# Self attention of layer 0: the values of fifteen elements from seven block products instead of eight

## The chip, the cores and the metric

The kernel runs on one core of a Trainium2 chip. The metric is the device time of one execution in microseconds; times shown are medians of several executions. Besides these there is one profiled execution, whose trace tells when every instruction and every transfer ran. Its times count from the first instruction (the span).

## What is computed

A batch of 16 elements x, each 256 positions by 256 features in fp32, goes through two transformer layers. Each layer has a self attention, a cross attention and a feed-forward part, so there are six phases of 16 elements. The change touches only the first phase, the self attention of layer 0, and in it the matrix product that makes the values:

```python
def _attn(xq, ctx, wq, wkv, wo, bo):          # self attention: ctx is xq
    q = _heads(xq @ wq)
    k, v = jnp.split(ctx @ wkv, 2, axis=-1)   # v: 256 x 1024 for each element
    ...
    o = jnp.einsum('bhnm,bhmd->bhnd', softmax(q k^T / 8), v)
    return o @ wo + bo
```

For one element the values are [256 x 256] times [256 x 1024]: the normalized and modulated input, held transposed as hT, times wv.

## The kernel before

**Order.** Every engine's order is written out by hand: what a function issues for an engine runs on it in just this order. The main loop goes through steps; an attention element has two (s = 0 and s = 1), and each step takes care of two groups of four heads. In a step of layer 0 TensorE makes, for the next step, the keys and queries (`stage_rotary`, L82 by way of the helper `product`), then the weighted sums of the values (`layer0_sums`, L638), in step 0 the values of the next element (`layer0_values`), in step 1 the folded output product of the element before (`finish_folded`), and at last the scores of the next step (`stage_s`, L569).

**Values.** `layer0_values(nxt)` in step 0 makes eight block products of 128 x 128 by 128 x 512: two halves t of the positions, two halves of the 1024 columns, two halves k of the 256 features, the last two added up in PSUM. `product` splits each into four matmuls of 32 output rows, which run side by side; the profile records each of these as two matmuls and two weight loads. The four results stand in the PSUM banks 6, 7, 4 and 5, and ScalarE copies each to the tile v (L478).

**Banks.** The scores of a step write banks 0 to 3 (first group of heads) and then 4 to 7 (second group). Keys and queries of the first group use banks 0 and 1, those of the second 2 and 3; the weighted sums use 4 and 5.

**VectorE in step 0**, in order: `both` (L590, a sum of two parts of the exponentials, two SBUF inputs), a transpose (L596), `m` (L526, keys and queries times the rotary table, read from PSUM), more of the same, the row sums (L603), and then `prepare_moments(third)`: the statistics of the element three further on (L324 to L328; the last is `ve`). For a cross attention to come, `context_moments` does the same for the context.

**POOL (GpSimd)**, in order: `qk` (L534, from pairs of m; m has two buffers of each kind, so m of the next group waits for qk), in step 0 `scale` (L627) and part of `fold_inner` (L736), in step 1 `add_bias` (L423) and one half of hT of the element two further on (L397, `prepare_input`; ScalarE makes the other half, L396). Once in the phase, in step 1 of element 0, `fold_weights` (L727) makes five sums of wo for the folded output product.

**SP** issues all transfers. The output weights wo of a phase come from the pool tag "wo" with two buffers; those of the cross attention (wo_ca, 1 MB) are loaded in step 1 of element 1, in the part "early".

**Start.** Before the loop, element 0 is prepared and its values and scores made; then come the moments, transposes and inputs of elements 1 and 2, with `prepare_input(jobs[1])` as the last call.

## Time and profile before

| what | time, us |
| --- | --- |
| median of 3 runs | 2196.24 (2194.89 to 2197.59) |
| the profiled execution | 2198.64 |
| its span, first to last instruction | 2196.8 |
| granted TensorE clock over the span | 0.999 |
| one usual element of the first phase | 41.3 |
| values of one element, TensorE (160.00 to 166.98) | 6.98 |

How each engine is used in two usual elements, from the busy times of the stretches 77.4 to 118.7 and 118.7 to 160.0 (each of 41.3 us):

| engine | first stretch, us | second stretch, us |
| --- | --- | --- |
| PE (TensorE, matmuls) | 41.30 | 41.30 |
| PEld (TensorE, weight loads) | 26.26 | 26.29 |
| DVE (VectorE) | 34.71 | 31.82 |
| ACT (ScalarE) | 12.73 | 12.73 |
| POOL (GpSimd) | 27.76 | 25.71 |

A line of the timeline reads: start, duration, engine, source line, operation, output<-inputs, shapes, how often in a row; in brackets the idle time of the engine before it and what ended that. [...] In the list of waits a line reads: who <- whom, total us, how many, the longest.

### The profile page before, as it was taken

How to read it: one execution, taken by the hardware profiler on the slowest of the kernel's cores; microseconds unless marked ns; L12 is line 12 of the kernel's file. 1: busy time of each engine (PE TensorE's matmuls, PEld its weight loads, DVE VectorE, ACT ScalarE, POOL GpSimd, SP SyncE). 2: the span in 40 equal slices, each digit the busy share in tenths (PEclk: the TensorE clock that was granted, in tenths of full speed). 3: DMA queues.
4: the chain of work that ended last, by engine and by line, in shares of the span. 5: the costliest groups of instructions: out<-in, count | busy, mean ns of one | idle time of the engine just before them, and what ended most of it. 6: DMA issues, size and time to landing. Idle time of an engine off the chain costs nothing.

```text
span 2196.8 us, 110836 instructions
## 1 busy us (share of the span) xinstructions
PE 2180.7 (99%) x50505; PEld 1431.6 (65%) x50505; DVE 1660.6 (76%) x3120; ACT 837.5 (38%) x1307; POOL 1071.6 (49%) x1033
## 2 busy tenths in 40 slices
PE   9999999999999999999999999999999999999998
PEld 5666666666665666666665668776656656657887
DVE  5886776777788899888899876664777777777654
ACT  3323323323233333333323332234666666663322
POOL 3766656656657867676676752221222232222220
PEclk9999999999999999999999999999999999999999
DMA  6110110110132221221212123221221232223221
GB/s 192 47 39 22 24 40 23 24 41 22 26 85 72 67 65 35 47 54 40 60 35 59 26 71 88 46 54 29 62 43 42 55 93 59 62 52 86 61 62 37
DMA packets 309321, 117.83 MB, mean 54 GB/s; under 512 B 245652, under 2 KB 292073, under 8 KB 308713
## 3 DMA queue, kind: packets, MB, share of 16 engines
q1 hardware_dynamic: 308840, 110.64, 21.1%
q8 instruction: 397, 6.50, 1.2%
q14 instruction: 84, 0.68, 0.1%
HBM read 77.14 MB, written 33.29 MB: 50 GB/s over the span
## 4 chain that ended last, share of the span: by engine, by line
PE 91%; DVE 3%; POOL 2%; DMA 1%; issue 1%; SPq 0%; ACT 0%; DVEq 0%; POOLq 0%; ACTq 0%
PE banks L82 59%; PE banks L569 15%; PE banks L638 9%; PE banks L654 5%; PE banks L505 1%; PE banks L472 1%; DVE m L526 1%; POOL raw L627 1%; POOL qk L534 1%; DMA spread<-sums_seen 0%; POOL folded L736 0%; DMA sums_seen<-inv 0%; DVE both L590 0%; DVE rows L603 0%; DVE squares L596 0%
## 5 line engine op out<-in xcount | busy, mean ns | idle before, releaser
L581 ACT ACTIVATE pr<-banks 128x1024 f32<-128x1024 f32 x576 | 487.6, 937 | 416.7 <-PE banks L569 211.5
L534 POOL TENSOR_TENSOR qk<-m,m 128x512 f32<-128x512 f32 x256 | 347.5, 1377 | 307.7 <-DVE m L526 199.6
L526 DVE TENSOR_TENSOR m<-banks,rope 128x512 f32<-128x512 f32 x512 | 324.2, 679 | 86.4 <-POOL qk L534 80.8
L590 DVE TENSOR_TENSOR both<-pr 128x512 f32<-128x512 f32 x256 | 222.7, 884 | 107.7 <-ACT pr L581 107.4
L645 ACT COPY raw<-banks 128x512 f32<-128x512 f32 x128 | 75.1, 587 | 468.6 <-PE banks L638 443.3
L569 PE MATMUL banks<-qk 32*64 32x256 f32 x8192 | 241.4, 378 | 4.0 <-DVE x L753 2.8
L638 PE MATMUL banks<-pr,v 128*32 128x256 f32 x4096 | 233.2, 379 | 0.0
L569 PEld LDWEIGHTS banks<-qk 32*64 32x64 f32 x8192 | 184.9, 131 | 64.6 <-issue 28.7
L704 ACT ACTIVATE g<-banks,cols 128x256 f32<-128x256 f32 x256 | 106.4, 472 | 273.0 <-PE banks L82 261.4
L638 PEld LDWEIGHTS banks<-pr,v 128*32 128x32 f32 x4096 | 132.9, 110 | 88.6 <-ACT pr L581 0.7
L82 PE MATMUL banks<-folded_w,folded 128*32 128x128 f32 x5856 | 176.2, 273 | 1.7 <-POOL folded L736 1.1
L627 POOL TENSOR_TENSOR raw<-raw,spread 128x512 f32<-128x512 f32 x128 | 162.8, 1304 | 19.0 <-DMA spread<-sums_seen 17.7
L82 PEld LDWEIGHTS banks<-folded_w,folded 128*32 128x32 f32 x5856 | 164.0, 110 | 3.1 <-POOL folded L736 2.2
L596 DVE STREAM_TRANSPOSE squares<-both 128x1024 f32<-128x1024 f32 x128 | 159.4, 1245 | 4.4
L603 DVE TENSOR_REDUCE rows<-squares 128x32 f32<-128x1024 f32 x128 | 155.5, 1215 | 2.2
L689 POOL TENSOR_TENSOR oT<-oT,spread 128x256 f32<-128x256 f32 x64 | 45.7, 736 | 209.8 <-DVE spread L688 209.8
L654 PE MATMUL banks<-pr,wide_v 128*32 128x256 f32 x2048 | 134.4, 379 | 1.1 <-ACT pr L581 1.1
L82 PE MATMUL banks<-hT,wk_sa 128*32 128x256 f32 x2048 | 135.3, 382 | 0.0
L330 POOL TENSOR_TENSOR rstd<-ve,neg_half 128x2 f32<-128x2 f32 x95 | 73.3, 772 | 125.9 <-DVE ve L328 122.5
L423 POOL TENSOR_TENSOR x<-x,bo_b 128x256 f32<-128x256 f32 x96 | 73.2, 782 | 125.8 <-DVE xh L338 125.8
L82 PE MATMUL banks<-hT,wq_ca 128*32 128x256 f32 x2048 | 133.9, 379 | 0.0
L82 PE MATMUL banks<-hT,wq_sa 128*32 128x256 f32 x2048 | 133.9, 379 | 0.0
(162 smaller groups left out, 3667.0 us busy)
## 6 DMA issues: line engine op xcount, KB each, us to landing
turned<-blocks SPq DMA_DIRECT2D x380, 64.0 KB
fetched<-turned SPq DMA_DIRECT2D x380, 64.0 KB
spread<-sums_seen SPq DMA_DIRECT2D x128, 128.0 KB
x<-in_x SPq DMA_DIRECT2D x16, 256.0 KB
fetched_c<-turned_c SPq DMA_DIRECT2D x64, 64.0 KB
cT<-in_ctx_turned SPq DMA_DIRECT2D x16, 256.0 KB
out<-x SPq DMA_DIRECT2D x16, 256.0 KB
ctx<-in_ctx SPq DMA_DIRECT2D x16, 192.0 KB
```

Of the source, the lines that this page charges most:

```text
L82: nc.tensor.matmul(out[cut], lhsT[:, cut], rhs, start=start, stop=stop)
L526: nc.vector.tensor_tensor(m, pq, rope[:, s : s + 1, :].to_broadcast([P, 2, N]), ALU.mult)
L534: nc.gpsimd.tensor_tensor(r, x, y, (ALU.subtract, ALU.add)[out])
L569: nc.tensor.matmul(banks[64 * g : 64 * g + 64, at + h, t * N : (t + 1) * N], lhs, rhs, start=(half == 0), stop=(half == 1 or job["layer"] ...
L581: nc.scalar.activation(pr[:, one], sc[:, one], AF.Exp, scale=0.125 if job["layer"] == 0 else 0.25)
L590: nc.vector.tensor_tensor(job["both"][:, 2 * p : 2 * p + 2, :], pr[:, :, 0, :], pr[:, :, 1, :], ALU.add)
L596: nc.vector.transpose(job["squares"].rearrange("p b k -> p (b k)"), job.pop("both").rearrange("p h n -> p (h n)"))
L603: nc.vector.tensor_reduce(job["rows"][:, u, :], job.pop("squares"), AX.X, ALU.add)
L627: nc.gpsimd.tensor_tensor(part, part, spread[:, u : u + 1, :].to_broadcast([P, 2, N]), ALU.mult)
L638: nc.tensor.matmul(o[32 * h : 32 * h + 32, half, :], v[:, t, col : col + 32], prs[h // 2][:, h % 2, t, :], start=(t == 0), stop=(t == NT - 1),
L654: nc.tensor.matmul(o[32 * h : 32 * h + 32], v[:, t, 4 * c + h, 32 * e : 32 * e + 32], prs[h // 2][:, h % 2, t, :], start=(t == 0), stop=(t ...
L704: nc.scalar.activation(g[:, c, :], ph[:, c, :], AF.Gelu, bias=column(w["b1"], 2 * u + c))
```

## The change

The values of elements 1 to 15 are made by Strassen's method in Winograd's form. With a[t][k] the four 128 x 128 blocks of the input and b[k][h] the four 128 x 512 blocks of the weights, seven products give the four blocks of v:

- Once, before the loop, POOL makes four sums of the weights (`split_value_weights`, t1 to t4, each 128 x 512). They lie in a buffer of the tag "wo".
- For each element POOL makes four sums of the input blocks (`split_value_inputs`, s1 to s4, each 128 x 128): for element 1 before the loop, for the others in step 1, two elements ahead, right after `prepare_input(after)`.
- TensorE makes seven products (`split_values`) in place of eight. Four of them are added up one after another in bank 6 (main), and ScalarE copies what stands there after each of the four; between them stand the products into banks 4, 7 and 5.
- VectorE then adds those three banks to what ScalarE copied: four additions of 128 x 512 (`join`), called after the statistics of step 0.
- The load of wo_ca moves from step 1 of element 1 to step 1 of element 14, behind the values' weights of the cross attention, since its buffer now first holds the split weights.
- Element 0 and the cross attention keep `layer0_values`.

```diff
-    def product(out, lhsT, rhs, start, stop):
+    def product(out, lhsT, rhs, start, stop, read_between=False):
...
-            nc.tensor.matmul(out[cut], lhsT[:, cut], rhs, start=start, stop=stop)
+            nc.tensor.matmul(out[cut], lhsT[:, cut], rhs, start=start, stop=stop, skip_group_check=read_between)
...
             w["wv"] = wtile([P, 2, H * 64], "wv", f"wv_{kind}")
+            if kind == "sa":
+                w["split_v"] = wtile([P, 8, D], "wo", "split_v", 2)
...
+        if part == ("early" if kind == "sa" else "output"):
             w["wo"] = wtile([P, 8, D], "wo", f"wo_{kind}", 2)
             nc.sync.dma_start(out=w["wo"], in_=chunked(a[f"{kind}_wo"]))
...
+    def split_value_weights():
+        b = value_weights()
+        t1, t2, t3, t4 = phases[0]["split_v"] = [phases[0]["w"]["split_v"][:, 2 * i : 2 * i + 2, :].rearrange(
+            "p c d -> p (c d)") for i in range(4)]
+        nc.gpsimd.tensor_tensor(t1, b[0][1], b[0][0], ALU.subtract)
+        nc.gpsimd.tensor_tensor(t2, b[1][1], t1, ALU.subtract)
+        nc.gpsimd.tensor_tensor(t3, b[1][1], b[0][1], ALU.subtract)
+        nc.gpsimd.tensor_tensor(t4, b[1][0], t2, ALU.subtract)
+
+    def split_value_inputs(job):
+        if job["p"] > 0 or job["b"] == 0:
+            return
+        a = value_inputs(job)
+        t = work.tile([P, 4, P], F32, tag="value_sums", name=f"value_sums_{job['key']}", bufs=1)
+        s1, s2, s3, s4 = job["split_v"] = [t[:, i] for i in range(4)]
+        nc.gpsimd.tensor_tensor(s1, a[1][0], a[1][1], ALU.add)
+        nc.gpsimd.tensor_tensor(s2, s1, a[0][0], ALU.subtract)
+        nc.gpsimd.tensor_tensor(s3, a[0][0], a[1][0], ALU.subtract)
+        nc.gpsimd.tensor_tensor(s4, a[0][1], s2, ALU.subtract)
+
+    def split_values(job):
...
+        main, other, side, extra = (bank(i, 512) for i in (6, 7, 4, 5))
+        for at, left, right, first, kept in (
+            (main, a[0][0], b[0][0], True, v[0][0]), (side, s1, t1, True, None), (main, s2, t2, False, v[0][1]),
+            (other, a[0][1], b[1][0], True, None), (main, s3, t3, False, v[1][1]), (extra, s4, b[1][1], True, None),
+            (main, a[1][1], t4, False, v[1][0]),
+        ):
+            product(at, left, right, first, True, True)
+            if kept is not None:
+                nc.scalar.copy(kept, at)
+
+        def join():
+            for to, at in ((v[0][0], other), (v[0][1], side), (v[1][1], side), (v[0][1], extra)):
+                nc.vector.tensor_tensor(to, at, to, ALU.add)
+        return join
...
     prepare_input(jobs[1])
+    split_value_inputs(jobs[1])
+    split_value_weights()
     for i, (j, s) in enumerate(steps):
...
             load_phase(job["p"] + 1, "values")
+            if job["p"] == 0:
+                load_phase(1, "output")
...
+            joins = None
             if nxt["kind"] == "attn" and s == 0:
-                layer0_values(nxt)
+                if nxt["p"] == 0:
+                    joins = split_values(nxt)
+                else:
+                    layer0_values(nxt)
             if s == 0:
                 prepare_moments(third)
                 context_moments(third)
+                if joins:
+                    joins()
                 prepare_fetch(after)
             else:
                 prepare_norm(third)
                 prepare_context(third)
                 prepare_input(after)
+                split_value_inputs(after)
                 if job["b"] == 0:
                     fold_weights(job["phase"])
```

More of the change, by code (lines that the diff above doesn't have):

```diff
@@ L478, in layer0_values, with value_weights, value_inputs @@
                 nc.scalar.copy(job["v"][:, t, cut], pv)
+    def value_weights():
+        return [[phases[0]["w"]["wv"][:, k, h * 512 : (h + 1) * 512] for h in range(2)] for k in range(2)]
+    def value_inputs(job):
+        return [[job["kT"][:, k, t * P : (t + 1) * P] for k in range(2)] for t in range(2)]
+    def split_value_weights():
[6 more added lines that the diff above has]
+        nc.gpsimd.tensor_tensor(t4, b[1][0], t2, ALU.subtract)
@@ new lines, in split_values @@
+    def split_values(job):
+        a, b = value_inputs(job), value_weights()
+        s1, s2, s3, s4 = job.pop("split_v")
+        t1, t2, t3, t4 = phases[0]["split_v"]
+        job["v"] = work.tile([P, NT, H * 64], F32, tag="v", name=f"v_{job['key']}")
+        v = [[job["v"][:, t, h * 512 : (h + 1) * 512] for h in range(2)] for t in range(2)]
+        main, other, side, extra = (bank(i, 512) for i in (6, 7, 4, 5))
[11 more added lines that the diff above has]
+        return join
```

## The prediction

> **What bounds the kernel now.** I read the engine totals first, then the chain that ended last, then TensorE's own waits in the first 660 us (the self attention of layer 0), then the order of time around three of its elements.

> ```profile
> PE 2180.7 (99%) x50505; PEld 1431.6 (65%) x50505; DVE 1660.6 (76%) x3120; ACT 837.5 (38%) x1307; POOL 1071.6 (49%) x1033
> PE 91%; DVE 3%; POOL 2%; DMA 1%; issue 1%; SPq 0%; ACT 0%; DVEq 0%; POOLq 0%; ACTq 0%
> PE banks L136 <- POOL ones L95: 1.3, 1, 1.3
> PE banks L154 <- DMA rows<-in_rows: 0.2, 1, 0.2
> ```

> TensorE is the bound, and up to 660 us it waits for nobody but at the very start. So a product taken away there is worth its full time, and a new wait of TensorE costs its full time: there is no slack to absorb it.

> ```profile
> 160.00 7.05 PE L82 MATMUL banks<-wv_sa,hT 128*32 128x512 f32 x64
> 161.29 0.13 PEld L82 LDWEIGHTS banks<-wv_sa,hT 128*32 128x32 f32 x4 [0.30 <-issue]
> 161.72 0.13 PEld L82 LDWEIGHTS banks<-wv_sa,hT 128*32 128x32 f32 x4 [0.30 <-issue]
> 161.97 0.59 ACT L478 COPY v<-banks 128x512 f32<-128x512 f32 x1 [1.13 <-PE banks L82]
> 164.02 0.64 DVE L328 TENSOR_SCALAR ve<-mv 128x2 f32<-128x2 f32 x1
> 166.98 3.71 PE L569 MATMUL banks<-qk 32*64 32x256 f32 x128
> 170.16 1.92 DVE L590 TENSOR_TENSOR both<-pr 128x512 f32<-128x512 f32 x2 [5.50 <-ACT pr L581]
> ```

> This is a usual element (times from 160.00 on; the stretch of 41.3 us repeats). The eight products take 6.98. Each is 8 recorded matmuls in two quartets; weight loads come in quartets 0.4285 apart, each issued when the quartet before starts. VectorE has finished its statistics (ve) at 4.66 after the values' start and is then idle for 5.5: the room for the joins. Their deadline is the second half of the scores, which writes banks 4 to 7: it starts 1.8 into the scores, at 8.76 now.

> **The gain.** One product of eight: 2 x 0.4285 = 0.857 us in 15 elements, 12.9 us. The four ScalarE copies stay four.

> **Waits on the reused bank.** Products 3, 5 and 7 overwrite what a copy is still reading. From a main product's second quartet on: 0.61 until its last matmul ends (0.59 and three steps of 0.006), 0.07 until the copy starts (161.90 to 161.97), 0.586 the copy, 0.05 to the weight load that waits (VectorE's end at 685.75, TensorE at 685.80): 1.316. TensorE would be free after three quartets, at 1.286. It is 0.03 late, and a weight load that is not issued ahead adds some 0.03 (the first quartets after such a wait stand 0.03 to 0.05 further apart). Products 3 and 5 also wait for POOL's sums; a second wait in an instruction of its own cost 0.06 more in these rows (VectorE ends 684.73, matmul 684.88):

> ```profile
> 684.88 0.61 PE L569 MATMUL banks<-qk 32*64 32x256 f32 x2 [0.99 <-DVE x L753]
> 685.80 0.91 PE L569 MATMUL banks<-qk 32*64 32x256 f32 x24 [0.31 <-DVE x L757]
> ```

> So 0.05 to 0.14 a wait; I take 0.075, as it is open whether the copy's wait is the separate one: 45 x 0.075 = 3.4 us (2.3 to 6.3). A usual element then saves 0.857 - 0.225 = 0.63 before its scores, and the joins' deadline moves from 8.76 to 8.13.

> **The joins.** Four additions from PSUM, 128x512, like m (four in 2.54). ScalarE's copies and products 4 and 6 end before their turn (the third copy near 5.3). In a usual element: 4.66, plus 0.3 because POOL's first new sum slips between the two `both` additions (`both` took 0.91 beside POOL's hT and 0.69 without it), plus 2.54, plus 0.1 to TensorE: 7.6, half a microsecond before 8.13. Hidden by the 5.5 of idle time: 0 in 11 elements. Elements 14 and 15 also have the context's statistics there, which end at 6.01: 6.01 + 0.3 + 2.54 + 0.1 = 8.95, 0.8 late, twice: 1.6 us (1.0 to 2.6).

> **POOL's sums, and where they stand in the queue.** An input sum is 128x128. 128x512 takes 1.25 and 128x256 0.70 (four in 2.79), so the line gives 0.43 and four make 1.7; bounds: in proportion 0.32 each, 1.3, and as 128x256, 2.8. They run after hT of an element, where POOL next idles 5.7, so usually they are hidden (without that room qk, m and the joins would slip by the 1.7, and the joins' half microsecond with it). A weight sum is 1.26 alone (2.52 for two) and 1.43 beside VectorE (7.15 for five): 5.0, to 5.7. All eight stand, once, behind hT of element 1 and ahead of its qk:

> ```profile
> 37.19 0.95 POOL L397 TENSOR_SCALAR hT<-fetched,fac_a,add_a 128x256 f32<-128x256 f32 x1 [5.79 <-DVE m L526]
> 38.11 2.52 POOL L534 TENSOR_TENSOR qk<-m,m 128x512 f32<-128x512 f32 x2
> 39.42 2.54 DVE L526 TENSOR_TENSOR m<-banks,rope 128x512 f32<-128x512 f32 x4 [1.71 <-POOL qk L534]
> 46.53 0.17 DVE L328 TENSOR_SCALAR ve<-mv 128x2 f32<-128x2 f32 x1
> 49.15 3.71 PE L569 MATMUL banks<-qk 32*64 32x256 f32 x128
> ```

> qk slips by 6.7 (6.3 to 8.5). VectorE's m waits for qk's buffers, and behind m in VectorE's queue stand the reductions, the statistics and the joins: 46.70 + 6.7 + 2.54 + 0.1 = 56.05 at TensorE, where the second scores would start at 49.15 + 1.82 - 0.63 = 50.34. **Loss 5.7** (5.3 to 7.5). The products themselves have their operands in time (t4 near 45, used at 47.5).

> The next element has a queue that is late already, for fold_weights stands ahead of qk, and now four input sums ahead of that:

> ```profile
> 69.53 7.15 POOL L727 TENSOR_TENSOR folded_w<-wo_sa 128x512 f32<-128x512 f32 x5
> 76.64 2.52 POOL L534 TENSOR_TENSOR qk<-m,m 128x512 f32<-128x512 f32 x2
> 77.37 7.05 PE L82 MATMUL banks<-wv_sa,hT 128*32 128x512 f32 x64
> 85.06 0.63 DVE L328 TENSOR_SCALAR ve<-mv 128x2 f32<-128x2 f32 x1
> ```

> The statistics end 8.32 after the values' start; plus 1.7 for the sums, less 0.35 that VectorE gains on TensorE during the first stall (its first m of the next step came 2.33 after the scores' end, and needs only 1.97 for TensorE's product), plus 2.54 and 0.1: 12.3 against 8.13. **Loss 4.2** (3.8 to 5.3). From the third element on the stall itself has given POOL its time back.

> [...]

> **What is moved.** wo_ca (1 MB) is issued at element 14 behind wv_ca instead of at 80.9 us, since its buffer first holds the split weights. Both wait on SP's queue for the same last products (wv_ca now leaves at 621.60). Behind them SP next issues turned at 644.14; at the span's mean 54 GB/s the megabyte takes 19 us and is through by then, and its first reader is POOL at 727.5: 0. If it were not, turned would come up to a few us late against hT, which is wanted an element later. The flag of the product helper issues nothing.

> **Sum.** -12.9 + 3.4 + 5.7 + 4.2 + 1.6 = +2.0 us on the profiled span of 2196.8, 2198.8; that execution took 2198.64 in all, 1.8 outside the span, and stands 2.4 above the median 2196.24 of the runs shown. The forecast for the median is 2196.24 + 2.0 = 2198.3. With every cost at its low end -0.5, at its high end +8.8: 2195.7 to 2205.0 for this case alone.

> **Rivals.**
> - Joins late in every element (slower). Place: the second scores of the 11 usual elements. It decides from 0.5 us of lateness on. For it: `both` may be held by two of the new sums rather than one (0.75 instead of 0.3), and four separate 0.69 additions with a wait each make 3.0 instead of 2.54: 4.66 + 0.75 + 3.0 + 0.1 = 8.5, 0.4 late, 11 x 0.4 = 4.4, and some 2.2 more in the other four: +8.6, 2204.8. Against: m keeps its 0.61 step beside POOL.
> - POOL's new work is covered (faster): no stall in elements 1 and 2, 2.0 - 9.9 = -7.9, 2188.4. For it: POOL idles 5.79 just before 37.19, and wv_sa is there since 21 us. Against: the sums stand behind hT in program order, and qk follows hT at once.
> - The copies are the bound (slower): 0.25 a wait, 45 x 0.25 = 11.3 instead of 3.4, +9.9, 2206.1. For it: nothing is spare on that path (0.03 short as it is), and ScalarE copies raw just before. Against: that copy ends at 160.85, before the first one can start.

> **How the numbers follow.** The case of the sum 0.60, joins late 0.16, covered 0.12, copies 0.12. Within 0.2% (about what a measurement here can tell from no change) is 2191.9 to 2200.6. The first case ends there with 0.40, above with 0.19, below with 0.01; joins late is above with 0.15; covered is below with 0.11; copies above with 0.10; the rest within. Faster 0.12, same 0.44, slower 0.44; the time is that of the likeliest case, so no change that can be told. The range 2190 to 2207 reaches into the rivals on both sides and leaves out about 2 in 10.

> **What will show it.** Right: seven products in about 6.35 us per element; TensorE waiting on VectorE's new line about 5 and 4 us in elements 1 and 2, under 1 in 14 and 15, and not at all between; three waits on ScalarE's copies of some 0.1 each; POOL's first qk near 45 instead of 38. Wrong: no wait at 50 us, qk near 38, waits on the joins in every element, or gaps of 0.25 and more between the products.

## The result, and the profile after

The changed kernel takes 2203.18 us (median of 9 runs, 2200.66 to 2204.58) against 2196.24 us (9 runs, 2194.61 to 2197.59): a ratio of 1.0031, 95% interval 1.0021 to 1.0041, so 6.9 us slower. The forecast was 2198.3 with a range of 2190 to 2207. Its profiled execution took 2204.2 us, with a span of 2202.4 and a mean granted clock of 0.998. The functions below the change have moved down: scores are L627 now (L569 before), qk is L592, m L584, both L648, ve L331, the sums of inputs L511 to L514, those of the weights L500 to L503, the copies of the products L531 and the joins L535.

First the busy times and the chain that ended last, from the page:

```profile
PE 2178.8 (99%) x50385; PEld 1435.3 (65%) x50385; DVE 1706.6 (77%) x3180; ACT 836.8 (38%) x1307; POOL 1116.9 (51%) x1097
PE 89%; DVE 4%; POOL 3%; DMA 2%; issue 1%; SPq 1%; ACT 0%; DVEq 0%; POOLq 0%; ACTq 0%
```

TensorE has 120 matmul records less and is still the bound, but its share of the chain fell from 91 to 89%: VectorE, POOL and a transfer each have a point more. TensorE's own waits up to 660 us (who, whom, total us, how many, longest) say where:

```profile
PE banks L627 <- DVE v L535: 8.1, 2, 4.7
...
PE banks L82 <- POOL split_v L500: 0.7, 1, 0.7
PE banks L627 <- DVE m L584: 0.6, 1, 0.6
...
PE banks L82 <- POOL split_v L501: 0.3, 1, 0.3
```

Two waits of the scores on the joins, and three small ones before the first of them (on sums of the weights and on m). None of these was there before. The timeline of element 1, all engines, from the landing of its input to the next keys:

```profile
39.86 0.60 ACT L399 ACTIVATE hT<-fetched,add_a,fac_a 128x256 f32<-128x256 f32 x1 [6.09 <-DMA fetched<-turned]
40.61 0.47 POOL L511 TENSOR_TENSOR value_sums<-hT 128x128 f32<-128x128 f32 x1
...
43.72 1.06 PE L82 MATMUL banks<-split_v,value_sums 128*32 128x512 f32 x8 [0.71 <-POOL split_v L500]
...
47.45 2.52 POOL L592 TENSOR_TENSOR qk<-m,m 128x512 f32<-128x512 f32 x2
...
48.76 2.53 DVE L584 TENSOR_TENSOR m<-banks,rope 128x512 f32<-128x512 f32 x4 [11.26 <-POOL qk L592]
...
55.86 0.17 DVE L331 TENSOR_SCALAR ve<-mv 128x2 f32<-128x2 f32 x1
55.94 2.48 DVE L535 TENSOR_TENSOR v<-banks,v 128x512 f32<-128x512 f32 x4
...
57.98 4.15 PE L627 MATMUL banks<-qk 32*64 32x256 f32 x64 [4.66 <-DVE v L535]
...
62.06 1.07 PE L82 MATMUL banks<-hT,wk_sa 128*32 128x256 f32 x16
```

This is read from top to bottom: POOL's eight sums take 6.84 (40.61 to 47.45), VectorE has stood idle for 11.26 until qk frees its buffers, its statistics end at 55.86, the joins follow, and the second half of the scores starts at 57.98. The last two rows show something more: that half takes 4.08 (57.98 to 62.06; its row's 4.15 runs 0.07 into the next), where the same work took 1.86 before. Some of that is a wait inside it: it starts after the third of the four joins, and goes on in earnest 0.55 later, when the fourth has ended (58.42). The table of stretches of 5 us (busy times of PE, PEld, DVE, ACT and POOL, then the granted clock, the third number from the end) shows the rest:

```profile
50.00:55.00 5.00, 2.72 (x64) 1.50 (x60) 4.93 (x7) 2.09 (x3) 2.50 (x2) 1.00 0.00 0
55.00:60.00 5.00, 2.02 (x34) 1.29 (x42) 4.93 (x12) 0.34 (x1) 0.70 (x1) 0.85 0.00 0
60.00:65.00 5.00, 5.00 (x102) 2.77 (x90) 1.77 (x3) 1.94 (x2) 0.00 (x0) 0.81 0.01 3
```

TensorE's clock fell. The trace's clock records put it at 0.5 from 58.52 to 61.94, and once more from 99.48 to 102.90, after the second wait; before the change no such record stands between 15 and 2192 us. The second wait is in element 2 (timeline of POOL, VectorE and TensorE, and the stretch of 5 us with the lowest clock):

```profile
80.47 7.16 POOL L785 TENSOR_TENSOR folded_w<-wo_sa 128x512 f32<-128x512 f32 x5
87.59 2.52 POOL L592 TENSOR_TENSOR qk<-m,m 128x512 f32<-128x512 f32 x2
...
96.49 2.47 DVE L535 TENSOR_TENSOR v<-banks,v 128x512 f32<-128x512 f32 x4
...
98.51 3.84 PE L627 MATMUL banks<-qk 32*64 32x256 f32 x64 [3.43 <-DVE v L535]
102.27 1.35 PE L82 MATMUL banks<-hT,wk_sa 128*32 128x256 f32 x16
```

```profile
100.00:105.00 5.00, 5.00 (x94) 2.71 (x82) 2.84 (x3) 1.94 (x2) 4.26 (x4) 0.71 0.02 5
```

And a usual element, in order of time:

```profile
174.04 1.04 PE L82 MATMUL banks<-wv_sa,hT 128*32 128x512 f32 x8
...
174.90 2.05 PE L82 MATMUL banks<-split_v,value_sums 128*32 128x512 f32 x16
...
175.15 0.59 ACT L531 COPY v<-banks 128x512 f32<-128x512 f32 x1 [0.27 <-PE banks L82]
...
176.74 1.07 PE L82 MATMUL banks<-wv_sa,hT 128*32 128x512 f32 x8
...
178.22 0.61 DVE L331 TENSOR_SCALAR ve<-mv 128x2 f32<-128x2 f32 x1
...
178.74 2.47 DVE L535 TENSOR_TENSOR v<-banks,v 128x512 f32<-128x512 f32 x4
...
180.49 3.71 PE L627 MATMUL banks<-qk 32*64 32x256 f32 x128
```

The joins end at 181.21, before the second half of the scores needs their banks, and the scores run through in 3.71, as before: the joins are hidden. The products take 6.45 (174.04 to 180.49) instead of 6.98. The element's period is 40.79 instead of 41.32.

The time by which the changed kernel's trace lags behind that of before, at the values of one element after another, is -0.2 at element 1, +9.3 at element 2, +14.6 at element 3, then 0.53 less with each element down to +8.8 at element 14, and +9.6 at 652, when the phase ends. In the profiled pair 3.2 us of it go again in the next phase and 0.7 behind it, though the change leaves all work there as it was. That part differs between executions anyway: experiment 4 has a kernel that does there what the kernel before does, and gains 2.9 in the same phase.

### The profile page after: what moved, and what is told of

Read it like the earlier page. It is cut to its first block, busy times and chain, and to the rows that moved or that the text cites. A ratio compares the mean times of both kernels' runs of the same rounds, so it can differ in the third digit from the quotient of the medians.

```text
span 2202.4 us, 110782 instructions
## 1 busy us (share of the span) xinstructions
PE 2178.8 (99%) x50385; PEld 1435.3 (65%) x50385; DVE 1706.6 (77%) x3180; ACT 836.8 (38%) x1307; POOL 1116.9 (51%) x1097
## 4 chain that ended last, share of the span: by engine, by line
PE 89%; DVE 4%; POOL 3%; DMA 2%; issue 1%; SPq 1%; ACT 0%; DVEq 0%; POOLq 0%; ACTq 0%
PE banks L82 58%; PE banks L627 15%; PE banks L696 8%; PE banks L712 5%; PE banks L563 1%; DVE m L584 1%; PE banks L475 1%; POOL qk L592 1%; DMA x<-in_x 1%; DVE rows L661 1%; POOL raw L685 0%; DVE squares L654 0%; DVE both L648 0%; SPq L210 0%; POOL folded L794 0%
## 5 line engine op out<-in xcount | busy, mean ns | idle before, releaser
L592 POOL TENSOR_TENSOR qk<-m,m 128x512 f32<-128x512 f32 x256 | 348.1, 1380 | 269.5 <-DVE m L584 257.2
L584 DVE TENSOR_TENSOR m<-banks,rope 128x512 f32<-128x512 f32 x512 | 324.2, 679 | 97.1 <-POOL qk L592 87.7
L648 DVE TENSOR_TENSOR both<-pr 128x512 f32<-128x512 f32 x256 | 228.7, 904 | 57.7 <-ACT pr L639 57.0
L627 PE MATMUL banks<-qk 32*64 32x256 f32 x8192 | 247.6, 381 | 11.2 <-DVE v L535 8.1
L627 PEld LDWEIGHTS banks<-qk 32*64 32x64 f32 x8192 | 186.7, 132 | 75.6 <-issue 35.6
L82 PE MATMUL banks<-folded_w,folded 128*32 128x128 f32 x5856 | 175.3, 273 | 0.5 <-POOL folded L794 0.5
L82 PEld LDWEIGHTS banks<-folded_w,folded 128*32 128x32 f32 x5856 | 164.2, 110 | 1.0 <-POOL folded L794 1.0
L82 PE MATMUL banks<-hT,wk_sa 128*32 128x256 f32 x2048 | 135.5, 381 | 0.0
L82 PE MATMUL banks<-hT,wq_sa 128*32 128x256 f32 x2048 | 134.3, 379 | 0.0
L82 PE MATMUL banks<-hT,wq_ca 128*32 128x256 f32 x2048 | 133.9, 379 | 0.0
```

The source lines that it names most:

```text
L82: nc.tensor.matmul(out[cut], lhsT[:, cut], rhs, start=start, stop=stop, skip_group_check=read_between)
L584: nc.vector.tensor_tensor(m, pq, rope[:, s : s + 1, :].to_broadcast([P, 2, N]), ALU.mult)
L592: nc.gpsimd.tensor_tensor(r, x, y, (ALU.subtract, ALU.add)[out])
L627: nc.tensor.matmul(banks[64 * g : 64 * g + 64, at + h, t * N : (t + 1) * N], lhs, rhs, start=(half == 0), stop=(half == 1 or job["layer"] ...
L648: nc.vector.tensor_tensor(job["both"][:, 2 * p : 2 * p + 2, :], pr[:, :, 0, :], pr[:, :, 1, :], ALU.add)
```

## The experiments

Each ratio is against the kernel before, run beside it on the same chip. Its medians were 2196.43 (for the experiments 1 to 4), 2195.14 (5 to 7 and the first part of 8) and 2195.87 (the second part of 8, 9 and 10). The diffs are cut to the lines that matter.

**1. The weights' sums first in POOL's queue.**

```diff
+    split_value_weights()
     prepare_input(jobs[1])
     split_value_inputs(jobs[1])
-    split_value_weights()
```

> The four sums of the weights ahead of hT of element 1, where POOL idles some 6 to 9 us. Theory (the loss sits where POOL's sums stand in its queue): the first qk starts 5 us earlier, near 42.4 if hT lands as late as in the trace of the change and near 40 if it lands as before; TensorE's wait for the joins of element 1 falls from 6.4 us to 1 to 3.5, the slow stretch after it goes or shrinks; element 2 keeps its wait of 3.5. Time 2194.5 to 2198. Rival A (the loss is spread over all elements, by the waits between the products and the joins): no more than 1 us better, 2202 to 2203. Rival B (the loss of the start comes from hT's late transfer): qk moves, but TensorE still waits 5 us or more in element 1; 2201 to 2203.

Measured: 2198.66, ratio 1.0007 (0.9998 to 1.0016), just above the expected 2194.5 to 2198. TensorE's waits on the joins:

```profile
PE banks L627 <- DVE v L535: 4.5, 3, 3.5
```

The longest is element 2's; element 1's is down to 0.8, and no product waits for POOL. The clock stays at full speed after the wait of 0.8, and is at 0.5 from 91.04 to 94.45, at the end of that of 3.5. So the place of the sums made the first loss, and this edit doesn't touch the second.

**2. The folded weights a step earlier.**

```diff
             if s == 0:
...
                 if joins:
                     joins()
+                if job["p"] == 0 and job["b"] == 0:
+                    fold_weights(job["phase"])
...
-                if job["b"] == 0:
+                if job["b"] == 0 and job["p"] > 0:
                     fold_weights(job["phase"])
```

> fold_weights of the first phase moved from step 1 of element 0 to the end of its step 0, where POOL idles 10 us; the weights' sums stay where they are. Theory: element 1 keeps its wait of 6 us, element 2 loses its 3.5 us and the slow stretch behind it (2.2): 2196.5 to 2198. Rival A: under 1 us better, 2202 to 2203.

Measured: 2198.16, ratio 1.0007 (0.9998 to 1.0016), just above the expected 2196.5 to 2198. Its waits:

```profile
PE banks L627 <- DVE v L535: 4.9, 2, 4.7
PE banks L82 <- POOL split_v L500: 2.1, 1, 2.1
```

Now element 2 has none of note, and element 1 keeps its own. There the input landed late against the values (hT 0.65 before them; 2.11 in the changed kernel's trace), the second product waited 2.1 for t1, and the clock was at 0.5 for 6.83 us (54.19 to 61.01). The two losses are separate, and each comes from what stands ahead of qk on POOL.

**3. All of it moved.** Weights' sums first; the input sums of element 1 behind the first pair of qk of step 0; folded weights early; the joins ahead of the context's statistics:

```diff
...
             rotary(then, 0, 1)
+            if i == 0:
+                split_value_inputs(jobs[1])
...
                 prepare_moments(third)
-                context_moments(third)
                 if joins:
                     joins()
+                context_moments(third)
```

> Weights' sums ahead of hT, input sums of element 1 behind the first pair of qk, fold_weights early, joins ahead of the context's statistics. Theory: no wait in elements 1 and 2 beyond 1.5 us, none in 14 and 15, no drop of the clock; what stays is 0.53 us gained in each of 15 elements: 8 us less 0 to 1.5, so 2188 to 2190.5, faster than before by 0.26 to 0.37%. Rival A: 2200 or more.

Measured: 2189.41, ratio 0.9965 (0.9951 to 0.9978), faster than both kernels. TensorE's waits after the start of the kernel:

```profile
PE banks L627 <- POOL qk L592: 0.3, 1, 0.3
```

The list has no wait on a join. Short ones remain inside the second halves of the scores, which take 2.07, 2.15 and 2.14 in the elements 1, 2 and 15, against 1.86. There is no clock record below 1 in the phase. The joins and sums are the same as in the change; only their places differ.

**4. Control.** The edit of experiment 2 in the kernel before.

> The kernel before with fold_weights moved as in the second run, a control: TensorE never waited there, so by the theory nothing changes: 2196.2 within 1.5 us. If it gains 3 us or more, the gain of the second run is not the change's own.

Measured: 2197.27, ratio 1.0006 (0.9997 to 1.0015): no change, so the folded weights' early place is worth nothing by itself.

**5. Seven of eight products in the kernel before.**

```diff
+                skip = job["p"] == 0 and job["b"] > 0 and t == 1 and cut is halves[1]
-                for k in range(1 if job["cross"] else 2):
-                    product(pv, kT[:, k, t * P : (t + 1) * P], w["wv"][:, k, cut], k == 0, k == 1)
+                for k in range(1 if job["cross"] or skip else 2):
+                    product(pv, kT[:, k, t * P : (t + 1) * P], w["wv"][:, k, cut], k == 0, k == 1 or skip)
```

This leaves out the second half of the features in one quarter of the values.

> The kernel before with seven of the eight products of the values in elements 1 to 15 and nothing else changed; left out is one product (second half of the positions, second half of the columns, second half of the features), so that quarter of the values lacks half of its sum. Theory (TensorE is the bound, a product is worth its full time): 15 x 0.857 = 12.9 us less, 2183.4 (2182 to 2184.8). Rival (part of the product's time was cover for another engine, which then becomes the bound): less than 11 us gained, above 2185.4, with a new wait of TensorE in each element.

Measured: 2182.75, ratio 0.9947 (0.9934 to 0.9961), 12.4 us between the medians. The period of the usual element is 40.46 instead of 41.32, and TensorE waits for nobody up to 640 us but at the start. A product is worth its full time; this is the ceiling for any seven-product form here.

**6. No reuse of the bank**, on the version of experiment 3: the main products start the banks 0, 1, 2 and 6 (the adding up is left out).

> The version with the sums, the folded weights and the joins moved, and each of the four main products starts a bank of its own (0, 1, 2 and 6), so that none waits for the copy of the one before; left out is the adding up in bank 6, so the values are not those of the reference. Theory (the reused bank costs 0.34 us an element, by the wider spacing at products 3, 5 and 7): 15 x 0.34 = 5.0 us less than that version's 2189.4, 2184.4 (2183.2 to 2185.6), all quartets 0.429 apart but where a product waits for POOL's sums. Rival (the wider spacing is the separate wait on POOL's sums at products 3 and 5 alone): 45 waits lose nothing, some 1 us less, 2188 to 2189.5. The rival's mixture, half and half: 2187.

Measured: 2183.98, ratio 0.9951 (0.9938 to 0.9965): 11.2 us below its kernel before, where the version of experiment 3 stood 7.0 below, so 4.2 against the 5.0 expected; its second halves of the scores take 2.38 and 2.42 in the elements 1 and 2, 0.6 more in all than in experiment 3. In the trace every pair of neighbouring quartets stands 0.43 apart, and the period is 40.46, that of seven products with nothing else. Products 1 to 4 of one element, first here:

```profile
158.91 1.04 PE L82 MATMUL banks<-wv_sa,hT 128*32 128x512 f32 x8
159.76 1.90 PE L82 MATMUL banks<-split_v,value_sums 128*32 128x512 f32 x16
161.48 1.04 PE L82 MATMUL banks<-wv_sa,hT 128*32 128x512 f32 x8
```

and then in the version of experiment 3:

```profile
159.44 1.04 PE L82 MATMUL banks<-wv_sa,hT 128*32 128x512 f32 x8
160.30 2.05 PE L82 MATMUL banks<-split_v,value_sums 128*32 128x512 f32 x16
162.14 1.07 PE L82 MATMUL banks<-wv_sa,hT 128*32 128x512 f32 x8
```

The fourth product starts 2.57 after the first without the reuse, 2.70 with it: 0.13 for the copy that product 3 waits for.

**7. The last sum's product second**, on the version of experiment 3, so that one wait covers all of POOL's sums (the banks of s4's and s1's products change places as well, and the join of s4's product comes first):

```diff
...
-            (main, a[0][0], b[0][0], True, v[0][0]), (side, s1, t1, True, None), (main, s2, t2, False, v[0][1]),
-            (other, a[0][1], b[1][0], True, None), (main, s3, t3, False, v[1][1]), (extra, s4, b[1][1], True, None),
+            (main, a[0][0], b[0][0], True, v[0][0]), (extra, s4, b[1][1], True, None), (main, s2, t2, False, v[0][1]),
+            (other, a[0][1], b[1][0], True, None), (main, s3, t3, False, v[1][1]), (side, s1, t1, True, None),
...
```

> The version with the sums, the folded weights and the joins moved, and the product with s4, the last sum that POOL makes, stands second instead of sixth, so one wait covers all of POOL's input sums and products 3 and 5 wait for the copy alone. Theory (a second wait in an instruction costs some 0.06 us more, in products 3 and 5): 0.12 x 15 = 1.8 us less than that version, 2187.6 (2186.6 to 2188.8). Rival (the copy's lateness alone sets the 0.12 and 0.14 us): no change, 2189.4 (2188.4 to 2190.4).

Measured: 2186.89, ratio 0.9963 (0.9949 to 0.9977). The spacing after products 3, 5 and 7 begins is 0.459, 0.459 and 0.460 (0.553, 0.568, 0.477 before), and the period 40.62: 0.17 less in 14 elements, more than expected. In element 1 the second product waited 1.7 for the last sum, which eats most of it. So a wait on the copy alone costs 0.055 (0.030 before the second quartet, 0.024 before the next). At products 3 and 5 the further wait on POOL made it 0.07 and 0.08 more; product 7, which waits for no sum of POOL in either version, came 0.02 closer too, so not all of that is shown to be the wait.

**8. Idle products in the two waits** of the changed kernel, to keep TensorE busy (their result isn't used):

```diff
             for e in range(2):
+                if e and i in (1, 3):
+                    for _ in range(5 if i == 1 else 3):
+                        product(bank(6, 512), value_inputs(at0[0])[0][0], value_weights()[0][0], True, True)
                 stage_s(at0[0], 2 * at0[1] + e, 4 * e)
```

> The changed kernel, and between the two halves of the scores TensorE also makes five products (step 1 of the loop, the values of element 1's successor stall) and three products (the same place an element later) of 128x128 by 128x512 into bank 6 that nobody reads; each is 0.86 us, so 4.3 and 2.6 us of the waits of 4.66 and 3.43 us are filled with work. Theory (half of the loss beyond the waits is the granted clock, which falls to 0.5 for 3.41 us after a long wait of TensorE): the joins end when they did, the second half of the scores then runs at the full clock, 1.8 us instead of 4.08 and 3.8: 4.2 us less than the changed kernel, 2199.0 (2198.0 to 2200.2), and no row of the clock below 1 near 58 and 99 us. Rival (the second halves are slow for another reason, such as banks still being read or the joins' SBUF traffic): they keep 4.08 and 3.8, 2203 (2201.8 to 2204.5). Second rival (the added work delays the scores itself): above 2204.5.

Measured: 2201.25, ratio 1.0029 (1.0018 to 1.0041), above the expected 2198.0 to 2200.2, while its profiled execution took 2198.31. As trace and median did not agree, both kernels ran once more, side by side:

> The changed kernel itself, unaltered, beside the next one on the same chip. Expected: 0.2 to 0.4% above the kernel before, as measured (1.0031); in its trace both waits for the joins, in the elements 1 and 2, the granted clock at 0.5 for 3.41 us or twice that after each, and the wait of element 1 the longer the later hT of element 1 lands (39.86 us gave 4.66 + 0.60 and products that wait too; 37.95 gave 4.7 with the folded weights moved).

> The kernel with idle products in the two waits, unaltered, beside the changed kernel on the same chip and in the same call. Theory (the low clock costs what the trace of element 2 shows, 1.6 us at an equal wait, and 1.7 in element 1): 3.2 us below the changed kernel (2 to 4.4). Rival (the executions without a trace show no gain, since the idle products cost as much by holding the scores back in some of them): 0 to 1 us below it. In the trace: clock 1.00 around both waits; hT of element 1 near 37 us goes with a fast execution, near 39 to 40 with a slow one.

Measured: the changed kernel 2204.00, ratio 1.0033 (1.0020 to 1.0046); with idle products 2201.32, ratio 1.0027 (1.0017 to 1.0036). TensorE's timeline in the latter, and its stretch from 55 to 60 us:

```profile
51.30 4.50 PE L82 MATMUL banks<-wv_sa,hT 128*32 128x512 f32 x40
56.03 2.49 PE L627 MATMUL banks<-qk 32*64 32x256 f32 x64 [0.23 <-DVE v L535]
58.45 1.07 PE L82 MATMUL banks<-hT,wk_sa 128*32 128x256 f32 x16
```

```profile
55.00:60.00 5.00, 4.77 (x103) 2.48 (x99) 3.93 (x6) 1.37 (x2) 0.00 (x0) 1.00 0.02 3
```

The clock stays at 1.00 and the second half takes 2.42, not 4.08. It doesn't come down to the expected 1.8, since inside it TensorE still waits 0.56 for the last join: of the 2.22 by which that half was longer in element 1, the clock made 1.66. Element 2 allows the cleanest comparison, as its second half starts equally late in both (11.91 and 11.87 after the values): its period is 45.03 with idle products and 46.61 without. So the low clock costs some 1.6 in each of the two elements, 3.2 in all, and not the 4.2 expected. The timed runs bear that out where both kernels ran side by side (8.1 and 5.5 above the kernel before, 2.7 apart), and less in the earlier runs (6.9 and 6.1, 0.8 apart); with executions that spread over 4 to 5 us, how much of the 3.2 reaches the median stays open. One source of that spread is on record: with idle products the two profiled executions, whose hT of element 1 started at 36.93 and 37.92, were the fastest of their runs (2198.31 and 2199.35), while the changed kernel's two, at 39.86 and 39.72, lay above their medians (2204.2 and 2206.08). So the profiled pairs set an early landing against a late one, and only comparisons inside an element, like the two above, are free of that.

**9. Only the two moves of experiments 1 and 2 together.**

> The changed kernel with only two moves: the weights' four sums stand ahead of hT of element 1 in POOL's queue, and the folded weights are made at the end of step 0 of element 0. The input sums and the joins stay where the change put them. Theory (the two waits and the two drops of the clock come from POOL's queue alone): no wait over 1.1 us in element 1, none in element 2, no row of the clock below 1, 0.2 to 0.9 us in the elements 14 and 15; 11 us below the changed kernel and 4 us below the kernel before (2.5 to 5.5). Rival (the version with four moves needed the other two as well): a wait of 2 us or more remains in element 1 or 2, and the time is within 2 us of the kernel before.

Measured: 2190.30, ratio 0.9974 (0.9965 to 0.9983): 5.6 below the kernel before, where 2.5 to 5.5 was expected. Its one profiled execution has a span of 7997.6, so its waits can't be read. By the times, the two moves alone turn the loss into a gain. The other two moves of experiment 3 (7.0 below its kernel before) account for at most little: the two intervals overlap.

**10. The best version**: experiment 7, but element 1 keeps the change's order of products, and the folded weights are made in two parts, clear of `both`.

```diff
...
             rotary(then, 1, 1)
+            if i == 0:
+                fold_weights(job["phase"], (1, 3, 4))
...
                 split_value_inputs(after)
-                if job["b"] == 0 and job["p"] > 0:
-                    fold_weights(job["phase"])
+                if job["b"] == 0:
+                    fold_weights(job["phase"], (1, 3, 4, 6, 7) if job["p"] > 0 else (6, 7))
```

> The version with the last sum's product second, with two further moves: element 1, whose last input sum comes late, keeps the order of the change for its products (that product waited 1.9 us for POOL), and the five folded weights are made in two parts, three right behind the first step's qk and two in the next step behind the input sums, clear of the additions `both` of VectorE. Theory: 1.7 us less in element 1 and 0.5 to 1 us less in the step after it, so 2.4 us below that version, which stood 8.2 us below the kernel before: 10.6 us below the kernel before (9 to 12). Rival (the step after element 1 is held by something else than the folded weights): 9.5 to 10 us below.

Measured: 2186.01, ratio 0.9954 (0.9941 to 0.9967), 9.9 below the kernel before, against 10.6 expected; that lies in the range of the rival (9.5 to 10) as well as in that of the theory (9 to 12), so it doesn't decide between them. The wait on the last sum in element 1 is gone, and the period of element 1 is 35.59 instead of experiment 7's 36.93; in the elements 1 and 2 the second halves of the scores now wait for the joins and take 2.78 and 2.85 (1.86 without a wait), and the period of element 2 is 41.61 instead of 41.06. This is the fastest complete version of the study, though its interval overlaps those of experiments 3 and 7.

## Where the prediction was right, and what it left out

The measured time lies in the range, but not because the terms were right: what was wrong with them went almost all in one direction, and the range held it since it had been drawn wide for the rivals. So the hit owes something to luck. The table sets each term against the pair of traces, up to the end of the phase.

| term | predicted, us | measured, us |
| --- | --- | --- |
| one product less, 15 elements | -12.9 | -12.9 |
| waits on the reused bank | +3.4 | +5.0 (0.336 an element) |
| joins in the usual elements | 0 | 0 |
| element 1 | +5.7 | +10.0 |
| element 2 | +4.2 | +5.8 |
| elements 14 and 15 | +1.6 | +1.5 (0.57 and 0.89) |
| sum | +2.0 | +9.4 (the traces: +9.8 from element 1 to 652 us) |

**Gain.** Right: TensorE is the bound, and experiment 5 shows the product worth its full time.

**Waits on the reused bank.** The mechanism is right: experiment 6 takes it away, and 0.33 an element goes. The size, 0.075 a wait, was too small: 0.12, 0.14 and 0.07 at products 3, 5 and 7. The working said that products 3 and 5 also wait for POOL's sums and that a second wait had cost 0.06, and then took a value near the low end. Experiment 7, which does without that second wait, gives half of the cost back (0.17 an element). +1.6 on the sum.

**Joins.** Right. In a usual element they end 7.2 after the values' start (predicted 7.6) and the second half of the scores starts at 8.2 (predicted 8.13); in the elements 1 and 2 the experiments 1 to 3 show that they are late by what delays VectorE ahead of them.

**Element 1.** The chain was named as it came: POOL's eight sums take 6.84 (predicted 6.7) ahead of qk, m waits, and the statistics and the joins stand behind. Two things made 5.7 into 10.0.
- The landing of hT: some 2.6, what is left of the 4.3 without the clock. hT came 2.77 later than in the working, and the chain behind it was 0.29 shorter. The working started at 37.19, POOL's row in one execution; in the changed kernel's that row stands at 39.96. Over the 13 profiled executions of this study whose trace can be read, ScalarE's half of that hT started between 36.92 and 39.86 us, 38.2 in the mean. The kernel does not set it: the two with idle products are the changed kernel up to that point, and had 36.93 and 37.92 where the changed kernel had 39.86 and 39.72. In the five traces that keep the change's queue in element 1 the second half of the scores starts 18.09 to 18.47 after it, wherever the values began, so the changed kernel hands a late landing on in full. The kernel before does not: with one product left out and hT at 39.16 (experiment 5) TensorE waited for nobody. The length of the chain was right: the working had 18.96 from ScalarE's half of hT (37.09) to TensorE's start after the fourth join (56.05); in the trace that is 18.67 (39.86 to 58.53). Part of the lateness is met earlier: products 2 and 3 wait for t1 and t2, and the scores start 1.4 later for it; "The products themselves have their operands in time" had looked at t4.
- The clock, 1.66.

**Element 2.** With the fourth join's 0.56 the wait is worth 4.2, just as predicted (the fourth join ends 12.3 after the values' start, as worked out). The other 1.6 is the clock again, as experiment 8 shows.

The records also tell when the drop comes. The two of the changed kernel's trace begin 40.96 apart, 12 times 3.413, and so do the two of its second execution (57.71 and 98.67); the waits before them end 40.53 apart in the first of these traces (57.98 and 98.51). In the 3.413 us ahead of each of the six drops of the phase (in four traces) TensorE worked 0 to 28% of the time; after a stretch of that length with 47% (51.70 to 55.11 in the changed kernel) the clock stayed full. Between the two nothing was measured, but that after one of 45% a low clock stayed low (experiment 2, 54.19 to 57.60).

**Sum.** The table's 9.4 is for an execution in which hT landed 1.7 later than the mean of the 13; with the mean it would be 7.7, an estimate, as both profiled executions of the changed kernel landed late. So the forecast's +2.0 lacked 1.6 for the bank, some 1.0 for a usual landing and 3.2 for the clock, and had 0.1 too much in the elements 14 and 15. The timed +6.9 is 0.8 below the 7.7; that is less than the next phase alone varies from one execution to another (3.2 in the profiled pair), and it wasn't pursued. The moved load of wo_ca is at nothing, as predicted: it is issued at 630.0, first read at 734.5, and nothing waits for it.

**Rivals.** "Joins late in every element" fell (3.71 for the scores). "POOL's new work is covered" fell as put, but came nearly true once the sums and the folded weights stood elsewhere: 2189.41 in experiment 3, 2188.4 in the rival. "The copies are the bound" has its mechanism (0.336 an element) and not its size (0.75). And "no change that can be told" fell by a little: the ratio's interval begins at 1.0021.

## What to carry to other kernels

Work that is made once may still stand in the one place where it delays everything behind it: look for the queue position before pricing the work, and for the idle stretch a few microseconds earlier in the same queue (here 1.0031 became 0.9974 by two moves of unchanged instructions). Where TensorE is the bound, look up the granted clock around a long wait before pricing it as idle time alone: each wait of 3.4 to 4.7 us here came with a stretch at half clock (in the changed kernel 1.6 us more for each), and those up to 2.1 us with none. And where a new chain starts at a transfer, take the spread of its landing over several executions and not the one row of a profile.

## What the runs showed of the hardware

- TensorE's six waits of 3.4 to 4.7 us (3.43, 3.44 and 3.46; three of 4.66), two in each trace of the changed kernel and one each in the experiments 1 and 2, came with a granted clock of 0.5: for 3.413 us in five cases, for 6.827 in experiment 2. Waits of 0.8 (experiment 1), 1.7 (experiment 7) and 2.1 us (experiment 2) had no record below 1. With idle products in the wait (experiment 8) it stayed at 1.00.
- Four of the drops came 2.80 to 5.20 us after the wait began: in the changed kernel 0.5 and 1.0 us after TensorE was back at work (57.98 and 58.52; 98.51 and 99.48), in experiment 1 just before (91.04; back at 91.14), in experiment 2 in the middle of the wait (54.19; idle from 51.39 to 56.05). So the wait and its price can stand on different lines of a profile. The two drops of one trace began 40.96 apart, 12 times 3.413, in both traces that have two.
- Where a matmul waited for a copy that was all but done (experiment 7), the two gaps around it were 0.030 and 0.024 wider; with a further wait in the same place, on POOL's sums that had long been made (experiment 3), the cost was 0.07 to 0.08 more (0.02 of which came at product 7 too, without such a wait).
- Beside POOL's folded weights, made early (experiment 3, 48.38 to 55.51), `both` of VectorE, which reads two SBUF tiles, was slow: two took 3.05 (1.28 at 58.34 in the changed kernel's trace, with POOL idle). The joins beside them, which read one operand from PSUM, kept their step (four in 2.48).
